# Summing the keys of a causal attention: totals folded from 128 rows to 32 by accumulating transfers, and one TensorE pass for four of them

## The chip, the cores and the metric

The kernel runs on one core of one Trainium2 chip. The metric is the device time of one execution in microseconds (us). Engines are named as in the profile: PE is TensorE, PEld its weight loads, DVE is VectorE, ACT is ScalarE, POOL is GpSimd, SP is SyncE, whose queue issues most transfers. PEclk is the clock granted to PE as a share of full speed.

## The reference

For 32 batches of 256 channels by 32x32 pixels: a group norm with 32 groups, then causal attention over the 1024 pixels with 8 heads of 32, added to the input.

```python
def reference(x, q_w, q_b, kv_w, kv_b):            # x (32, 256, 32, 32), float32
    xf = group_norm(x).reshape(B, C, S)            # 32 groups, eps 1e-5; S = 1024
    q = einsum('oc,bcs->bos', q_w, xf) + q_b       # 8 heads of 32 channels
    kv = einsum('oc,bcs->bos', kv_w, xf) + kv_b
    k, v = kv[:, :256], kv[:, 256:]                # ... to (B, 8, S, 32)
    mask = tril(ones((S, S)), -1)                  # strictly before: the centre is hidden too
    scores = where(mask == 0, -10000.0, einsum('bhqd,bhkd->bhqk', q, k) / sqrt(32))
    attn = where(mask == 0, 0.0, softmax(scores))
    return x + einsum('bhqk,bhkd->bhqd', attn, v)
```

## The kernel before

Scores are computed transposed, so that keys lie on the 128 partitions and queries along the free axis. ACT takes the exponential, POOL zeroes what the mask hides, PE multiplies with the values, and DVE adds up the exponentials of all key blocks into a running total of 128 x 4 heads x 512 queries. The softmax's denominator is the sum of that total over its 128 partitions. PE makes it with a matrix of ones (`pick`): four column blocks, one for each head of a group. A batch has four such totals (two groups of four heads, two halves of the queries; `n` counts them).

```python
        def sum_keys(pd, e, cols, of, start=True, stop=True):
            for j in range(4):
                nc.tensor.matmul(
                    pd[HD * j : HD * (j + 1), of], lhsT=pick, rhs=e[:, j, cols],
                    start=start, stop=stop, skip_group_check=True,
                )
        # ... (cut)
        def sums(b, g, hf):
            n = NH * g + hf
            total = live.pop(("sum", b, g, hf))
            # ... (the last batch's last total is cut)
            pd = misc(f"pd_{b}_{n}")
            sum_keys(pd, total, slice(0, HALF), slice(0, HALF))
            den = small.tile([P, HALF], F32, tag="den", name=f"den_{b}_{n}")
            # ... (cut)
            nc.scalar.copy(den, pd)
            if n == 0:
                live["sums", b] = dram.tile([4, 4, HALF], F32, tag="sums", name=f"sums_{b}")
            nc.sync.dma_start(out=live["sums", b][n], in_=den[::HD, :])
```

The sums go to DRAM and come back as 128 rows of 64 (`gather`), are checked and inverted, and go to DRAM and back once more, now broadcast over the 32 channels of each head (`invert`). Then DVE finishes the batch: numerator times inverse, plus bias and input.

```python
            for n in ns:                                            # in invert()
                g, hf = divmod(n, NH)
                nc.sync.dma_start(
                    out=live["rb", b][:, g, hf * HALF : (hf + 1) * HALF],
                    in_=live["inv", b][n].unsqueeze(1).broadcast_to([4, HD, HALF]),
                )
```

The order of work is laid down by hand in visits, `N = 12` to a batch. A visit does the scores of one pair of tiles, then the functions put down for it in `at`, then the values of the visit before, then the functions in `after`. POOL, PE, ACT and DVE run in exactly that order.

```python
        PREPARE = (-22, -21, -20, -19, -18, -16, -11, -11)
        SUMS = (3, 7, 9, 13)
        FINISH = (N + 7, N + 7, N + 8, N + 9)
        # ... (cut)
                if b >= 2:
                    when(max(first - 2 * N - 1, 0), lambda b=b: load(b))
                    prepare(b, [first + n for n in PREPARE])
                for n in every:
                    # ... (cut)
                    when(v, lambda b=b, n=n: sums(b, *divmod(n, NH)), after)
                if not last:
                    when(first + N + 2, lambda b=b: gather(b, every))
                    when(first + N + 4, lambda b=b: check_sums(b, every))
                    when(first + N + 4, lambda b=b: invert(b, every))
                    for n in every:
                        when(first + FINISH[n], lambda b=b, n=n: finish(b, n), after)
```

Buffers: the exponentials that become totals have three buffers of two tags each (`e0` for the first block of a total, which also holds the total), input tiles four, and one PSUM bank (`misc`) serves the key sums and the norm's small products in turn.

## Time and profile before

| | before |
|---|---|
| median of 3 runs | 1958.25 us (1957.0 to 1959.33) |
| span of the profiled run, mean PEclk | 1956.8 us, 0.998 |
| period of a batch | 60.1 us |
| PE idle in the whole span | 21.3 us (1956.8 - 1935.5) |

The table of stretches of the kernel before; columns are busy us (and instructions) of PE, PEld, DVE, ACT and POOL, then PEclk, the mean busy share of the 16 DMA engines, and GB/s:

```profile
400.00:1900.00 1500.00, 1500.00 (x18750) 746.06 (x18746) 1208.18 (x1234) 1137.28 (x1446) 455.56 (x374) 1.00 0.16 54
...
```

In the steady part PE does not stop for one microsecond in 1500, at full clock, and the DMA engines are nearly empty. The same table for two microseconds within a batch, while the four broadcasts of inverses, issued from 1068.64, are running:

```profile
1072.00:1074.00 2.00, 2.00 (x30) 0.95 (x24) 1.90 (x2) 1.34 (x2) 2.00 (x1) 1.00 0.26 100
...
```

The share stands at 0.24 to 0.29 from 1070 to 1080: a quarter of the engines' time, for ten microseconds, at some 100 GB/s. The packet records of the same trace say how: from 1070 to 1080 four packets of the broadcasts are in flight at a time, which fits four engines at work and twelve at rest.

### The profile page before, as it was taken

How to read it: one execution, taken by the hardware profiler on the slowest of the kernel's cores; microseconds unless marked ns; L12 is line 12 of the kernel's file. 1: busy time of each engine (PE TensorE's matmuls, PEld its weight loads, DVE VectorE, ACT ScalarE, POOL GpSimd, SP SyncE). 2: the span in 40 equal slices, each digit the busy share in tenths (PEclk: the TensorE clock that was granted, in tenths of full speed). 3: DMA queues.
4: the chain of work that ended last, by engine and by line, in shares of the span. 5: the costliest groups of instructions: out<-in, count | busy, mean ns of one | idle time of the engine just before them, and what ended most of it. 6: DMA issues, size and time to landing. Idle time of an engine off the chain costs nothing.

```text
span 1956.8 us, 54680 instructions
## 1 busy us (share of the span) xinstructions
PE 1935.5 (99%) x24130; PEld 964.7 (49%) x24130; DVE 1553.9 (79%) x1604; ACT 1463.6 (75%) x1865; POOL 586.0 (30%) x498
## 2 busy tenths in 40 slices
PE   8999999999999999999999999999999999999997
PEld 4454554554544545545455445454454544544543
DVE  4787887888878878888778788787887887888768
ACT  5777777777777777777777777777777777777775
POOL 1332322323323323233232232332332322323223
PEclk9999999999999999999999999999999999999999
DMA  3011111111111111111111111111111111111002
GB/s 106 3 67 42 51 57 57 67 66 38 50 53 67 68 41 52 50 64 67 50 48 53 55 67 68 36 57 47 67 67 41 52 53 61 67 57 47 32 29 78
DMA packets 56539, 107.73 MB, mean 55 GB/s; under 512 B 14064, under 2 KB 15216, under 8 KB 56296
## 3 DMA queue, kind: packets, MB, share of 16 engines
q1 hardware_dynamic: 54520, 103.26, 14.8%
q8 instruction: 191, 3.13, 0.7%
q10 hardware_dynamic: 1776, 0.92, 0.2%
q14 instruction: 52, 0.43, 0.1%
HBM read 68.54 MB, written 35.62 MB: 53 GB/s over the span
## 4 chain that ended last, share of the span: by engine, by line
PE 97%; DVE 2%; DMA 1%; ACT 0%; issue 0%; ACTq 0%; SPq 0%; DVEq 0%
PE sT L267 30%; PE acc L337 25%; PE pp L159 24%; PE ppv L159 12%; PE pd L351 6%; DVE e L342 0%; DMA wn<-in_L_conv_kv_w_dram 0%; DMA x<-in_x_dram 0%; DVE rb L439 0%; PE pv L159 0%; DVE rb L422 0%; DVE rb L423 0%; PE pm L159 0%; ACT e L314 0%; ACT k L221 0%
## 5 line engine op out<-in xcount | busy, mean ns | idle before, releaser
L314 ACT ACTIVATE e<-sT 128x1024 f32<-128x1024 f32 x768 | 744.9, 1022 | 274.0 <-PE sT L267 227.6
L342 DVE TENSOR_TENSOR e<-e,eh 128x1024 f32<-128x1024 f32 x382 | 540.0, 1427 | 361.2 <-PE acc L337 341.1
L282 POOL TENSOR_SCALAR_AFFINE_SELECT e<-e 128x512 f32<-128x512 f32 (+1 forms) x256 | 392.9, 1535 | 1337.5 <-ACT e L314 1151.9
L342 DVE TENSOR_TENSOR e<-e,e 128x1536 f32<-128x1536 f32 x381 | 634.0, 1664 | 17.4 <-POOL e L282 3.0
L267 PE MATMUL sT<-q,k 32*128 32x256 f32 (+3 forms) x7168 | 617.5, 460 | 0.8 <-ACT k L221 0.8
L267 PEld LDWEIGHTS sT<-q,k 32*128 32x128 f32 x7168 | 463.6, 184 | 202.3 <-issue 105.6
L159 PE MATMUL pp<-xn,wT 128*32 128x512 f32 x4096 | 492.2, 598 | 0.0
L337 PE MATMUL acc<-e,v 128*32 128x512 f32 (+2 forms) x4096 | 400.7, 486 | 0.0
L315 ACT ACTIVATE eh<-sT 128x1024 f32<-128x1024 f32 x384 | 396.2, 1032 | 0.0
L159 PE MATMUL ppv<-wT,xn 128*32 128x256 f32 x4096 | 247.3, 382 | 0.0
L337 PEld LDWEIGHTS acc<-e,v 128*32 128x32 f32 x4096 | 132.6, 110 | 223.1 <-issue 200.7
L337 PE MATMUL acc<-eh,v 128*32 128x256 f32 x3072 | 224.4, 379 | 0.0
L159 PEld LDWEIGHTS pp<-xn,wT 128*32 128x32 f32 x4096 | 107.0, 109 | 218.2 <-issue 206.2
L382 ACT COPY den<-pd 128x512 f32<-128x512 f32 x126 | 73.9, 586 | 165.1 <-PE pd L351 165.1
L337 PEld LDWEIGHTS acc<-eh,v 128*32 128x32 f32 x3072 | 98.5, 110 | 164.2 <-issue 152.6
L159 PEld LDWEIGHTS ppv<-wT,xn 128*32 128x32 f32 x4096 | 120.2, 109 | 102.0 <-issue 32.1
L282 POOL TENSOR_SCALAR_AFFINE_SELECT eh<-eh 128x512 f32<-128x512 f32 x128 | 163.3, 1276 | 2.8
L351 PE MATMUL pd<-e,pick 128*32 128x512 f32 (+1 forms) x1048 | 136.7, 595 | 2.0 <-DVE e L342 2.0
L423 DVE SCALAR_TENSOR_TENSOR rb<-rb,v_bias_col,x 128x512 f32<-128x512 f32 (+1 forms) x127 | 95.4, 751 | 4.5
L221 ACT ACTIVATE q<-pp,qk_bias 128x512 f32<-128x512 f32 x128 | 89.9, 702 | 3.9 <-PE pp L159 3.9
L221 ACT ACTIVATE k<-pp,qk_bias 128x512 f32<-128x512 f32 x128 | 89.8, 702 | 2.2 <-PE pm L159 1.1
L346 ACT COPY num<-acc 128x512 f32<-128x512 f32 x128 | 76.4, 597 | 15.6 <-PE acc L337 15.6
(62 smaller groups left out, 526.2 us busy)
## 6 DMA issues: line engine op xcount, KB each, us to landing
x<-in_x_dram SPq DMA_DIRECT2D x64, 512.0 KB
out_dram<-rb SPq DMA_DIRECT2D x127, 256.0 KB
rb<-inverses SPq DMA_DIRECT2D x126, 256.0 KB
sums<-den SPq DMA_DIRECT2D x126, 8.0 KB
rows<-sums SPq DMA_DIRECT2D x31, 32.0 KB
inverses<-inv SPq DMA_DIRECT2D x31, 32.0 KB
wn<-in_L_conv_kv_w_dram ACTq DMA_DIRECT2D x2, 256.0 KB
wn<-in_L_conv_q_w_dram ACTq DMA_DIRECT2D x1, 256.0 KB
```

The costliest lines, as they stand in the source:

```text
L159: nc.tensor.matmul(out[part], lhsT=lhsT[:, part], rhs=rhs, start=start, stop=stop, skip_group_check=True)
L221: nc.scalar.activation(live[key][:, cols], pp, AF.Identity, bias=qk_bias[:, n, g : g + 1], scale=(SCALE, 1.0)[n],)
L267: ins = nc.tensor.matmul(pair[:, cols], lhsT=live["k", b, g][rows, kb * P : (kb + 1) * P], rhs=live["q", b, g][rows, hf * HALF + of.start ...
L282: nc.gpsimd.affine_select(out=diagonal, in_=diagonal, pattern=[[0, 4], [0, n], [1, P]], compare_op=ALU.is_gt, fill=0.0, base=0, channel_mu ...
L314: nc.scalar.activation(e[:, 2 * a : 2 * a + 2, :], pairs[a], AF.Exp)
L315: exp = nc.scalar.activation(eh.rearrange("p (n bank) q -> p bank n q", n=2), short, AF.Exp)
L337: nc.tensor.matmul(acc[HD * j : HD * (j + 1), of], lhsT=live["v", b][:, kb, h * HD : (h + 1) * HD], rhs=e[:, j, cols], start=first, stop=l ...
L342: nc.vector.tensor_add(total[:, :, of], total[:, :, of], e[:, :, cols])
L346: nc.scalar.copy(live["num", b][:, g, hf * HALF : (hf + 1) * HALF], acc)
L351: nc.tensor.matmul(pd[HD * j : HD * (j + 1), of], lhsT=pick, rhs=e[:, j, cols], start=start, stop=stop, skip_group_check=True,)
L382: nc.scalar.copy(den, pd)
L423: nc.vector.scalar_tensor_tensor(rb[:, g, cols], rb[:, g, cols], v_bias_col[:, g : g + 1], xt[:, g, cols], ALU.add, ALU.add)
```

## The change

The intent is to take three of the four PE groups of a batch away. GpSimd issues two transfers for each total that add its upper 64 rows to its lower 64, then the upper 32 of those to the lower 32 (`accum_op=ALU.add`). SP copies the 32 remaining rows into a stacked tile of 128 rows. With a matrix that picks by blocks of 32 rows (`pick_half`), one PE group sums all four totals at once. Everything behind moves later by three visits, and so do, to keep the buffers alive, the loads and the norm by two.

```diff
+        def fold(b, n, rows):
+            total = live["sum", b, *divmod(n, NH)]
+            nc.gpsimd.dma_start(out=total[:rows], in_=total[rows : 2 * rows], accum_op=ALU.add)
+
+        def stack(b, n):
+            if n == 0:
+                live["folded", b] = work.tile([P, 4, HALF], F32, tag="folded", bufs=1, name=f"folded_{b}")
+            total = live.pop(("sum", b, *divmod(n, NH)))
+            nc.sync.dma_start(out=live["folded", b][n * HD : (n + 1) * HD], in_=total[:HD])
+
+        def sum_folded(b):
+            pd = misc(f"pd_{b}")
+            sum_keys(pd, live.pop(("folded", b)), slice(0, HALF), slice(0, HALF), of_rows=pick_half)
+            # ... (copy to den, one write of 16 rows to DRAM)
 ...
-        PREPARE = (-22, -21, -20, -19, -18, -16, -11, -11)
+        PREPARE = (-20, -19, -18, -17, -16, -14, -11, -11)
-        FINISH = (N + 7, N + 7, N + 8, N + 9)
+        FINISH = (N + 10, N + 10, N + 11, N + 12)
 ...
-                    when(max(first - 2 * N - 1, 0), lambda b=b: load(b))
+                    when(max(first - 2 * N + 1, 0), lambda b=b: load(b))
 ...
+                        when(v, lambda b=b, n=n: fold(b, n, 2 * HD), after)
+                        when(v + 1, lambda b=b, n=n: fold(b, n, HD), after)
+                        when(v + 2, lambda b=b, n=n: stack(b, n), after)
 ...
-                    when(first + N + 2, lambda b=b: gather(b, every))
-                    when(first + N + 4, lambda b=b: check_sums(b, every))
-                    when(first + N + 4, lambda b=b: invert(b, every))
+                    when(first + N + 4, lambda b=b: sum_folded(b), after)
+                    when(first + N + 5, lambda b=b: gather(b, every), after)
+                    when(first + N + 7, lambda b=b: check_sums(b, every))
+                    when(first + N + 7, lambda b=b: invert(b, every))
```

(The last batch keeps its four groups.)

More of the change, by code (lines that the diff above doesn't have):

```diff
@@ L75, in tile_norm_attention_residual @@
     nc.gpsimd.memset(pick, 1.0)
+    pick_half = const.tile([P, 4, CPG], F32, name="pick_half")
+    nc.gpsimd.memset(pick_half, 1.0)
+    nc.gpsimd.affine_select(
+        out=pick_half, in_=pick_half, pattern=[[-HD, 4], [0, CPG]],
+        compare_op=ALU.is_ge, fill=0.0, base=0, channel_multiplier=1,
+    )
+    nc.gpsimd.affine_select(
+        out=pick_half, in_=pick_half, pattern=[[HD, 4], [0, CPG]],
+        compare_op=ALU.is_ge, fill=0.0, base=HD - 1, channel_multiplier=-1,
+    )
+    pick_half = pick_half.rearrange("p a b -> p (a b)")
     avg = const.tile([P, P // CPG, CPG], F32, name="avg")
@@ L346, in values, with sum_keys @@
                 nc.scalar.copy(live["num", b][:, g, hf * HALF : (hf + 1) * HALF], acc)
-        def sum_keys(pd, e, cols, of, start=True, stop=True):
+        def fold(b, n, rows):
[9 more added lines that the diff above has]
+            sum_keys(pd, live.pop(("folded", b)), slice(0, HALF), slice(0, HALF), of_rows=pick_half)
+            den = small.tile([P, HALF], F32, tag="den", name=f"den_{b}")
+            nc.scalar.copy(den, pd)
+            live["sums", b] = dram.tile([4, 4, HALF], F32, tag="sums", name=f"sums_{b}")
+            nc.sync.dma_start(out=live["sums", b].rearrange("j n c -> (j n) c"), in_=den[::CPG, :])
+        def sum_keys(pd, e, cols, of, start=True, stop=True, of_rows=pick):
             for j in range(4):
                 nc.tensor.matmul(
-                    pd[HD * j : HD * (j + 1), of], lhsT=pick, rhs=e[:, j, cols],
+                    pd[HD * j : HD * (j + 1), of], lhsT=of_rows, rhs=e[:, j, cols],
                     start=start, stop=stop, skip_group_check=True,
@@ L375, in sums @@
             den = small.tile([P, HALF], F32, tag="den", name=f"den_{b}_{n}")
-            if b == B - 1 and n >= 2:
+            if n >= 2:
                 most = small.tile([P, 1], F32, tag="most", name=f"most_{n}")
@@ L410, in invert @@
                 live["rb", b] = work.tile([P, NG, S], F32, tag="rb", name=f"rb_{b}")
+            by_half = live["inv", b] if b == B - 1 else live["inv", b].rearrange("j n c -> n j c")
             for n in ns:
@@ L414, in invert @@
                     out=live["rb", b][:, g, hf * HALF : (hf + 1) * HALF],
-                    in_=live["inv", b][n].unsqueeze(1).broadcast_to([4, HD, HALF]),
+                    in_=by_half[n].unsqueeze(1).broadcast_to([4, HD, HALF]),
                 )
@@ L432, in check_here @@
             least = small.tile([P, 1], F32, tag="least", name=f"least_{n}")
-            junk = small.tile([P, HALF], F32, tag="junk", bufs=1, name=f"junk_{n}")
+            junk = small.tile([P, HALF], F32, tag="den", name=f"junk_{n}")
             nc.vector.tensor_scalar(junk, live["den", n], SUM_MIN, 1.0, ALU.is_ge, ALU.min, accum_out=least)
@@ L549, in unshifted @@
                             when(first + i, lambda b=b, i=i: sum_pieces(b, products[i - 1], i == N - 1, i == N), after)
-                    when(v, lambda b=b, n=n: sums(b, *divmod(n, NH)), after)
+                    if last:
+                        when(v, lambda b=b, n=n: sums(b, *divmod(n, NH)), after)
+                    else:
+                        when(v, lambda b=b, n=n: fold(b, n, 2 * HD), after)
+                        when(v + 1, lambda b=b, n=n: fold(b, n, HD), after)
+                        when(v + 2, lambda b=b, n=n: stack(b, n), after)
                 if not last:
-                    when(first + N + 2, lambda b=b: gather(b, every))
-                    when(first + N + 4, lambda b=b: check_sums(b, every))
-                    when(first + N + 4, lambda b=b: invert(b, every))
+                    when(first + N + 4, lambda b=b: sum_folded(b), after)
+                    when(first + N + 5, lambda b=b: gather(b, every), after)
+                    when(first + N + 7, lambda b=b: check_sums(b, every))
+                    when(first + N + 7, lambda b=b: invert(b, every))
                     for n in every:
```

## The prediction

> **What bounds the kernel now.** I read first the page's busy shares, then the chain that ended last, then its costliest groups, to see which engine sets the pace and what part of it the change touches:
>
> ```profile
> PE 1935.5 (99%) x24130; PEld 964.7 (49%) x24130; DVE 1553.9 (79%) x1604; ACT 1463.6 (75%) x1865; POOL 586.0 (30%) x498
> ...
> PE 97%; DVE 2%; DMA 1%; ACT 0%; issue 0%; ACTq 0%; SPq 0%; DVEq 0%
> ...
> L382 ACT COPY den<-pd 128x512 f32<-128x512 f32 x126 | 73.9, 586 | 165.1 <-PE pd L351 165.1
> L351 PE MATMUL pd<-e,pick 128*32 128x512 f32 (+1 forms) x1048 | 136.7, 595 | 2.0 <-DVE e L342 2.0
> ```
>
> PE is busy for 99% of the span and is 97% of the chain, so time taken off PE comes off the end unless something else begins to make PE wait. The key totals (pd) are 1048 matmul instructions: 131 groups of eight (four column blocks, each product two instructions), almost one group per quarter of a batch. 136.7 us is their busy time, which overlaps their neighbours'. The chain in order of time counts what a group adds to the end; its summary gives 5.8% of 1956.8 us = 113.5 us, over 131 groups 0.87 us, and a single piece agrees:
>
> ```profile
> 1902.61 1.72 PE acc L337 x24
> 1904.33 0.86 PE pd L351 x8
> 1905.19 1.50 PE sT L267 x12
> ```
>
> A batch is 12 visits (scores of one visit, values of the one before, then extra work). The timeline of SP's queue shows its period, 1085.59 - 1025.48 = 60.1 us:
>
> ```profile
> 1025.48 5.69 SPq L428 DMA_DIRECT2D out_dram<-rb  x3
> ...
> 1036.63 1.81 SPq L106 DMA_DIRECT2D x<-in_x_dram  x2
> ...
> 1085.59 5.69 SPq L428 DMA_DIRECT2D out_dram<-rb  x3
> ```
>
> Less the four groups (3.5 us) and the two tiny norm groups that is about 4.67 us a visit, as the PE timeline also has it: visit 12 of a batch starts at 1043.39 and visit 13 at 1048.05.
>
> **What the Trainium skill says.** "DMA: Bandwidth & Descriptors", section "SWDGE vs HWDGE vs iDMA", has accumulation during a transfer only from GpSimd, which writes the descriptors in software; that is why the folds sit in GpSimd's queue, among the masks. The kernel before issues none there, so no row prices it. The same page, "Anatomy of one DMA", fits such a transfer as 2.0 us + bytes/436e3; for 512 KB that is 3.2 us, for 256 KB 2.6 us, without the accumulation. In the loop of this trace only SP issues transfers: the small write of the inverses, issued at 1067.03, let its reader issue at 1068.64, so 1.6 us there and back; and in one-microsecond windows the two 512 KB loads moved up to 418 GB/s, which agrees. "SBUF — State Buffer", section "Who interferes with whom", says that a DVE instruction with two SBUF inputs contends with a GpSimd instruction that reads SBUF but not with one that only writes. This trace agrees with the first half: one mask shape (128x512) took from 0.68 to 2.58 us in one batch. The second half says that the adds should not starve descriptor writing; no run here shows it yet. "TensorE: Matmul & The Clock Gate", Part 3, says that products in different column groups run together; a pd group of eight instructions of 0.59 us each lasts 1.04 us, which agrees, and the new pass keeps the form.
>
> **The change part by part.**
> 1. Removed from PE: of the 131 groups, 31 batches lose four and gain one. The compiled order has 93 fewer PE rows, one per group, and the last batch keeps its own. 93 x 0.87 = **81 us off the path**.
> 2. Removed from ACT: 93 copies of 586 ns, 54 us off an engine at 75%; beside the path. Four small writes to DRAM per batch become one of 16 rows, from SP, beside the path.
> 3. Added to GpSimd: 8 issues a batch, 248 in all. An issue costs an estimated 1 us (no row shows it; taken below the two-microsecond fixed part above): 8 us on 18.3 us of masks in a 57 us batch, far from full. Each second fold waits in GpSimd's order for the first to land. In the compiled order only the second folds of the first and third total have a mask before them and the next mask a visit behind; the others fall in the two-visit gap without masks (14 us idle in the trace). So masks should not be late.
> 4. Added to DMA: per total 512 + 256 KB of folding and 256 KB of stacking; 124 totals make 130 MB, on 107.7 MB now. The engines were 16% busy, so some 30 to 40%; not a bound, but the x loads and outputs now meet the folds.
> 5. Moved on DVE: the four finishes go from visits 7, 7, 8, 9 after the next batch starts to 10, 10, 11, 12, where adds already crowd. The DVE timeline in the stretch that produces the fourth total:
>
> ```profile
> 1032.47 2.36 DVE L342 TENSOR_TENSOR e<-e,eh 128x1024 f32<-128x1024 f32 x2 [1.65 <-PE acc L337]
> 1034.75 0.68 DVE L422 TENSOR_TENSOR rb<-num,rb 128x512 f32<-128x512 f32 x1
> 1035.46 0.75 DVE L423 SCALAR_TENSOR_TENSOR rb<-rb,v_bias_col,x 128x512 f32<-128x512 f32 x1
> 1036.13 2.29 DVE L342 TENSOR_TENSOR e<-e,e 128x2048 f32<-128x2048 f32 x1
> 1038.52 1.51 DVE L342 TENSOR_TENSOR e<-e,eh 128x1024 f32<-128x1024 f32 x1
> 1040.14 2.29 DVE L342 TENSOR_TENSOR e<-e,e 128x2048 f32<-128x2048 f32 x1
> 1042.53 1.93 DVE L342 TENSOR_TENSOR e<-e,eh 128x1024 f32<-128x1024 f32 x1
> 1044.57 3.24 DVE L342 TENSOR_TENSOR e<-e,e 128x1536 f32<-128x1536 f32 x2
> 1047.91 1.51 DVE L342 TENSOR_TENSOR e<-e,eh 128x1024 f32<-128x1024 f32 x1
> ```
>
> It is unbroken from 1032.47 to 1049.42. One finish (1.43 us) leaves it and three (each 1.43, with one 0.15 copy) enter ahead of the last add, +3.0 us: the fourth total ends near 1052.5 on this clock. PE's visit 14 would begin at 1048.05 + 4.67 = 1052.7 on the same clock, less the one removed group between them, 0.9 us. So the total is done about **0.7 us into visit 14**.
> 6. The new chain that PE waits for: first fold, second fold, stack, then the single pass after visit 16, 3 x 4.67 = 14.0 us after visit 14 starts. My estimates: first fold 1 us of issue + 1.3 to 2.6 us of movement (512 KB at 418 GB/s, or twice for reading the target too) + 1.5 us to be seen = 3.8 to 5.1; second 3.1 to 3.8; stack on SP 0.5 + 0.6 + 1.5 = 2.6. Sum 9.5 to 11.5, and 1 to 2.5 more where the 1 MB of x loads runs in the same microseconds: 10.5 to 14 after a start at 0.7. It fits with **0 to 3 us to spare**, on the edge; I put down 0.4 us a batch, 31 x 0.4 = 12 us.
> 7. The tail: from 1920.9 the chain is DVE alone, 31 us, with the finishes of batch 30 in it. Moving these later leaves DVE idle first and loaded after; up to the 6.1 us of four finishes is added, I take 5 us.
>
> Sum: 1958 - 81 + 12 + 5 = 1894; as the author's offsets look fitted to these waits, I shade it to **1890 us**.
>
> **The rivals.** (a) *The fold chain ends late and PE waits for the stacked tile.* For: the margin of step 6, the crowded DVE, one in-order SP queue that puts the stack behind outputs and loads. Against: the pass stands one visit after the stack. Each microsecond late costs 31 us; 2.6 us late eats the whole gain, so 1920 to 1990. (b) *GpSimd becomes the wait*: if an issue takes 3 us or more, or DVE starves it, masks come late, and PE has only some 1 to 2 us between a mask's end and the values that need it (a mask of visit 5 ends at 1015.60, PE uses it at 1016.53). Two late masks a batch of 1 us: 62 us, 1940 to 1950. (c) *DVE becomes the bound*: 1554/1890 = 82% on average, but visits 10 to 12 now carry about 6.9, 5.7 and 6.2 us in 4.67. It recovers in the light visits 13 to 15, and three buffers give about two visits of slack; so a few us at most. (d) *The gain is hidden anyway*: PE is 97% of the chain, so no. (e) Everything fits and the tail costs nothing: 1958 - 81 = 1877, or 1870 if a group is worth the 0.94 us that starts of neighbours differ by at one place.
>
> **Range and chances.** (e) is the floor, 1868. (a) and (b) in moderate form give the upper end, 1940. Faster by over 2% is below 1919: 36 us of losses beyond the 1877 + 5, 1.2 us a batch. I think three in four that the waits stay under it: 0.75; within 2%: 0.17; slower: 0.08.
>
> **What would show it.** Right: pd matmuls fall from 1048 to 304, den copies from 126 to 126 - 93 = 33, PE still above 97% and pd about 1.8% of the chain. Step 6: PE's idle before pd, released by the stacking transfer, is the loss; under 15 us in total confirms it, 80 us is rival (a). Step 3: idle of PE before values released by the masks on GpSimd is rival (b), and GpSimd's issues over 3 us. Step 5: the last add of the fourth total should end within visit 14. Step 7: the DVE chain at the end longer than 31 us. It would be wrong mainly through the duration of an accumulating transfer, which nothing in this trace measures.

## The result, and the profile after

| | before | after |
|---|---|---|
| median of 4 runs | 1958.79 us (1957.0 to 1959.45) | 2084.43 us (2073.88 to 2085.4) |
| profiled span, mean PEclk | 1956.8 us, 0.998 | 2082.7 us, 0.968 |
| PE idle in the span | 21.3 us | 162.9 us |
| period of a batch | 60.1 us | 59.8 to 65.2 us |

The change made the kernel slower: ratio 1.0631, 95% interval 1.0596 to 1.0666. A ratio here is always the mean time of one kernel's fast runs over the mean of the other's of the same rounds, so not quite the ratio of the medians. The prediction, 1890 us in 1868 to 1940, was wrong. The output was correct.

The page of the changed kernel: busy shares, the queue of the folds (packets, MB, share of 16 engines), the chain that ended last, a group, and two rows of issues (KB each, median us from issue to landing):

```profile
PE 1919.8 (92%) x23386; PEld 964.2 (46%) x23386; DVE 1567.8 (75%) x1604; ACT 1407.8 (68%) x1772; POOL 711.9 (34%) x749
...
q0 software_dynamic: 15872, 97.53, 33.8%
...
PE 44%; issue 22%; DMA 18%; POOL 9%; DVE 4%; ACT 3%; POOLq 0%; SPq 0%; ACTq 0%; DVEq 0%
...
L365 POOL DMA_DIRECT2D e<-e x248 | 204.1, 880 | 730.7 <-DMA e<-e 573.5
...
e<-e POOLq DMA_DIRECT2D x124, 512.0 KB, 8.6
...
e<-e POOLq DMA_DIRECT2D x124, 256.0 KB, 4.8
```

PE has fallen from 97% of the chain to 44%, and transfers carry 18%. The first folds land 8.6 us after their issue, the second ones 4.8 us (medians of all four totals). PE does 744 instructions less but is busy only 15.7 us less, which is odd for groups worth 81 us; the clock explains it below. PE's waits, with total us, times, and the longest:

```profile
PE pd L384 <- issue: 60.8, 18, 4.2
PE pd L384 <- DMA folded<-e: 40.1, 13, 4.2
PE acc L349 <- POOL e L294: 11.4, 28, 1.0
```

All 31 passes over the stacked tile wait (18 and 13), together 101 us. Where the label is "issue" the profile shows no releaser, but it is the same instruction, and it reads a tile that the stacking transfer fills. One batch shows the length of the road to it. On DVE the last add of the fourth total, then POOL's two folds of it, then SP with its neighbours, then PE (start, duration, engine and instruction, the idle time before and its releaser):

```profile
1044.08 2.14 DVE L354 TENSOR_TENSOR e<-e,eh 128x1024 f32<-128x1024 f32 x1
```

```profile
1046.52 0.89 POOL L365 DMA_DIRECT2D e<-e  x1 [1.38 <-DVE e L354]
1053.37 0.78 POOL L365 DMA_DIRECT2D e<-e  x1 [5.96 <-PE ppv L171]
```

```profile
1048.02 3.54 SPq L118 DMA_DIRECT2D x<-in_x_dram  x2
1058.92 0.51 SPq L371 DMA_DIRECT2D folded<-e  x1
```

```profile
1045.57 1.57 PE L279 MATMUL sT<-q,k 32*128 32x256 f32 x16
...
1058.99 0.61 PE L349 MATMUL acc<-eh,v 128*32 128x256 f32 x8
1063.03 1.23 PE L384 MATMUL pd<-folded,pick_half 128*32 128x512 f32 x8 [3.43 <-issue]
1064.20 3.09 PE L279 MATMUL sT<-q,k 32*128 32x256 f32 x24
```

The total is ready at 1046.22 and the first fold issued at 1046.52. The second fold follows 6.85 us later, the stack 5.55 us after that, and PE starts the pass 4.11 us after the stack: 16.5 us in all (medians of the 31 batches: 7.0, 5.0 and 4.5, and 16.4 from the first issue to the pass). PE was ready at 1059.60, 14.0 us after its visit 14 began at 1045.57. (POOL's second wait bears the name of a PE product; in other batches the same row, with the same length, names the first fold's landing.) Two more things are to be seen. The three transfers have neighbours: the loads of the next input are issued 1.5 us behind the first fold, and the first fold of the next batch's first total (at 1056.84, cut here) 2.1 us ahead of the stack. And after the gap, the score products that take 1.67 us elsewhere in this batch take 3.09 us. The table of stretches has the clock there (columns as before: busy us of PE, PEld, DVE, ACT and POOL, then PEclk, share, GB/s):

```profile
1063.80:1067.20 3.40, 3.40 (x28) 2.66 (x24) 3.00 (x5) 1.39 (x2) 0.00 (x0) 0.50 0.57 64
```

"TensorE: Matmul & The Clock Gate" of the Trainium skill, Part 1, "What's actually happening", has PE's clock drop to half after an idle window of about 3.4 us, free-running. The clock records of this trace agree with the half and with the free-running window: before the end of the program there are 21 stretches at 0.50, each 3.41 or 6.83 us long, and their starts lie whole multiples of 3.41 us apart. They do not show that the gap itself must be that long: 21 of the 31 gaps at the pass were followed by such a stretch, gaps from 2.8 to 4.2 us; the other gaps were 1.1 to 3.3 us (the ends of PE's instructions, and so the lengths of gaps, are modelled). The prediction did not have this term at all: a wait of this length can be paid twice.

At the end of the program, DVE of the changed kernel:

```profile
2044.78 0.22 DVE L433 SCALAR_TENSOR_TENSOR in_range<-rows,in_range 64x64 f32<-64x64 f32 x1 [12.65 <-DMA rows<-sums]
```

The last batch's small write of sums stands behind the late steps of the batch before it, and DVE waits 12.65 us for it; in the kernel before there is no such wait.

### The profile page after: what moved, and what is told of

It is laid out like the page before. It is cut to its first block, busy times and chain, and to the rows that moved or that the text cites. A ratio compares the mean times of both kernels' runs of the same rounds, so it can differ in the third digit from the quotient of the medians.

```text
span 2082.7 us, 53914 instructions
## 1 busy us (share of the span) xinstructions
PE 1919.8 (92%) x23386; PEld 964.2 (46%) x23386; DVE 1567.8 (75%) x1604; ACT 1407.8 (68%) x1772; POOL 711.9 (34%) x749
## 3 DMA queue, kind: packets, MB, share of 16 engines
q0 software_dynamic: 15872, 97.53, 33.8%
## 4 chain that ended last, share of the span: by engine, by line
PE 44%; issue 22%; DMA 18%; POOL 9%; DVE 4%; ACT 3%; POOLq 0%; SPq 0%; ACTq 0%; DVEq 0%
PE sT L279 15%; DMA e<-e 12%; PE acc L349 12%; PE pp L171 10%; POOL e L294 5%; PE ppv L171 5%; DMA folded<-e 4%; ACT e L326 3%; DVE e L354 2%; PE pd L384 2%; POOL e L365 2%; POOL rstd L209 1%; POOL eh L294 1%; DMA sums<-den 1%; DVE rb L457 1%
## 5 line engine op out<-in xcount | busy, mean ns | idle before, releaser
L354 DVE TENSOR_TENSOR e<-e,eh 128x1024 f32<-128x1024 f32 x382 | 509.3, 1347 | 382.0 <-PE acc L349 227.1
L279 PE MATMUL sT<-q,k 32*128 32x256 f32 (+3 forms) x7168 | 646.1, 477 | 0.9 <-ACT k L233 0.8
L279 PEld LDWEIGHTS sT<-q,k 32*128 32x128 f32 x7168 | 487.0, 193 | 183.1 <-issue 60.5
L294 POOL TENSOR_SCALAR_AFFINE_SELECT e<-e 128x512 f32<-128x512 f32 (+1 forms) x256 | 320.9, 1254 | 589.8 <-ACT e L326 580.3
L365 POOL DMA_DIRECT2D e<-e x248 | 204.1, 880 | 730.7 <-DMA e<-e 573.5
L349 PE MATMUL acc<-e,v 128*32 128x512 f32 (+2 forms) x4096 | 401.5, 487 | 11.4 <-POOL e L294 11.4
L294 POOL TENSOR_SCALAR_AFFINE_SELECT eh<-eh 128x512 f32<-128x512 f32 x128 | 145.8, 1139 | 4.6 <-ACT eh L327 3.6
L384 PE MATMUL pd<-folded,pick_half 128*32 128x512 f32 x248 | 44.2, 787 | 101.0 <-issue 60.8
L378 ACT COPY den<-pd 128x512 f32<-128x512 f32 x31 | 18.2, 586 | 153.2 <-PE pd L384 153.2
L456 DVE TENSOR_TENSOR rb<-num,rb 128x512 f32<-128x512 f32 (+1 forms) x127 | 115.5, 909 | 0.1
L457 DVE SCALAR_TENSOR_TENSOR rb<-rb,v_bias_col,x 128x512 f32<-128x512 f32 (+1 forms) x127 | 105.4, 830 | 4.5
```

The lines of the kernel that those rows point to most:

```text
L279: ins = nc.tensor.matmul(pair[:, cols], lhsT=live["k", b, g][rows, kb * P : (kb + 1) * P], rhs=live["q", b, g][rows, hf * HALF + of.start ...
L294: nc.gpsimd.affine_select(out=diagonal, in_=diagonal, pattern=[[0, 4], [0, n], [1, P]], compare_op=ALU.is_gt, fill=0.0, base=0, channel_mu ...
L349: nc.tensor.matmul(acc[HD * j : HD * (j + 1), of], lhsT=live["v", b][:, kb, h * HD : (h + 1) * HD], rhs=e[:, j, cols], start=first, stop=l ...
L354: nc.vector.tensor_add(total[:, :, of], total[:, :, of], e[:, :, cols])
L365: nc.gpsimd.dma_start(out=total[:rows], in_=total[rows : 2 * rows], accum_op=ALU.add)
L384: nc.tensor.matmul(pd[HD * j : HD * (j + 1), of], lhsT=of_rows, rhs=e[:, j, cols], start=start, stop=stop, skip_group_check=True,)
```

## The experiments

Twelve runs, each with rounds against the kernel before on the same chip. The first theory was: PE's wait for the stacked tile, with the slow clock behind it, is the loss (the prediction's rival (a)). Its rival: the rest of the change (transfers, masks, moved places) is.

### The pass without its wait

The stacked tile is still made, but PE sums a tile of ones instead, so the result is wrong.

```diff
-            sum_keys(pd, live.pop(("folded", b)), slice(0, HALF), slice(0, HALF), of_rows=pick_half)
+            live.pop(("folded", b))
+            for j in range(4):
+                nc.tensor.matmul(pd[HD * j : HD * (j + 1), :], lhsT=pick_half,
+                                 rhs=ones.broadcast_to([P, HALF]), start=True, stop=True, ...)
```

> The changed kernel, but the single pass reads a constant of ones instead of the stacked tile (a wrong result on purpose). All folds, stacks and their traffic stay; PE alone no longer waits for them. Theory A (PE's wait for the fold chain, with the slow clock after it, is the loss): the batch period falls from 63.8 us to about 60.1 - 2.6 = 57.5, plus some 0.4 us for one late mask; the clock is back at 0.99 or more; with the tail still some 19 us longer, 1958 - 81 + 19 + 12 = 1908 us. Theory B (traffic, GpSimd or DVE crowding slow the kernel by themselves): stays above 2000 us.

Measured: 1940.96 us (1934.39 to 1955.33), ratio 0.9935 (0.9893 to 0.9978), clock 0.991. All 101 us of waits are gone and the time falls by 143 us. So the wait and what follows from it make up nearly all of the loss. The expected 1908 was not reached: 33 us are lost otherwise. Of 29 periods 16 now take 57.9 to 58.1 us, which is the period of before, 60.1, less three groups of 0.87, plus about 0.4; **the removed groups are worth what the prediction said**. The other periods take 58.6 to 60.3 us and one 65.1 us, with a gap of 4.45 us in it; together they are 22 us above 57.9 each, and why is not known. The ends cost more, which the runs below show.

### The moved places alone

The kernel before with only the new places of loads, norm, gather, check, inversion and finishes; no fold, no stack, four groups. Correct.

```diff
-        PREPARE = (-22, -21, -20, -19, -18, -16, -11, -11)
+        PREPARE = (-20, -19, -18, -17, -16, -14, -11, -11)
-        FINISH = (N + 7, N + 7, N + 8, N + 9)
+        FINISH = (N + 10, N + 10, N + 11, N + 12)
   (load, gather, check_sums, invert moved as in the change)
```

> The kernel before with only the changed kernel's places of the later steps (loads and norm two visits later, gathering, checking, inverting and finishing three visits later); four PE groups a batch, no folds. Theory: the crowding of DVE by the moved finishes costs nothing in the steady state (PE busy 100% and a period of 60.1 us as before), but the end of the program grows, because the last batch's small write of sums now falls beside the broadcasts of the batch before it; in the changed kernel the time from the last single pass to the end was some 19 us longer. So 1970 to 1980 us, all of the increase after about 1890 us. Rival: the moved finishes delay PE every batch: PE idle in the middle, 1990 us or more.

Measured: 1993.32 us, ratio 1.0181 (1.0164 to 1.0198), above the expected band; the places alone cost 34.6 us. PE's waits name the first part, DVE's the second:

```profile
PE pv L159 <- ACT k L221: 11.7, 31, 0.4
```

```profile
DVE in_range L400 <- DMA rows<-sums: 12.4, 1, 12.4
```

Once a batch a tiny product of the norm (pv) now comes right behind a projection that holds the shared PSUM bank, and waits 0.38 us until ACT has emptied it: 12 us over the program. And the end stretches: with the batch before last finishing three visits later, its broadcasts stand ahead of the last batch's small write, and DVE waits 12.4 us. So, against the expectation, not all of the increase lies at the end: the key sum that PE starts at 1904.2 us in the kernel before starts at 1923.3 here, 19 us later, and 15 us more are lost behind it. (Beside the 12 us, PE waits six times in the steady part for the last add of a total, 4.4 us in all.) The mean clock, 0.994 where before has 0.998, adds little to it: of 24.7 us at half clock, all at the end, PE was busy in 3.5.

### Work for PE in the gap

Three groups whose result is overwritten, placed right ahead of the pass. Correct.

```diff
+            for _ in range(3):
+                for j in range(4):
+                    nc.tensor.matmul(pd[HD * j : HD * (j + 1), :], lhsT=pick, rhs=wT[:, 0, :HALF],
+                                     start=True, stop=True, skip_group_check=True)
             sum_keys(pd, live.pop(("folded", b)), ..., of_rows=pick_half)
```

> The changed kernel with three groups of useless matmuls (3 x 0.87 = 2.6 us) on PE in front of the single pass, into the same bank, which the pass then overwrites. They fill part of the wait and lengthen nothing where the wait is longer than 2.6 us. Theory: the wait of some 4 us empties PE long enough for the clock to drop, and the slow stretch after it costs about 60 us in all (mean clock 0.968 against 0.998). Filled, the clock stays at 0.995 or more, and the time falls to about 2020 to 2030 us although PE does more. Rival (the low clock is noise of the chip or has another cause): clock stays near 0.97 and the time at 2080 or above.

Measured: 2046.54 us (2043.81 to 2047.67), ratio 1.0452, clock 0.993. Giving PE 31 x 2.6 = 81 us **more** to do makes the kernel 38 us **faster** (medians; 36 by the means). The wait left at the pass is 22.7 us in sum (these and 1.2 named "issue"), the longest 2.0:

```profile
PE pd L390 <- DMA folded<-e: 21.5, 26, 2.0
```

No stretch at half clock is left before the end of the program, and the mean clock is 0.993 against 0.968. The useless groups take the place of 78 us of waiting almost one for one, so this shows the second payment: some 38 us of the loss are the slow clock after the gap. The time missed the expected 2020 to 2030 by 17 us and the clock the expected 0.995 by 0.002.

### Folds that copy instead of adding

The same transfers, from the same queue, without the accumulation. Its output is wrong, which doesn't matter for the time.

```diff
-            nc.gpsimd.dma_start(out=total[:rows], in_=total[rows : 2 * rows], accum_op=ALU.add)
+            nc.gpsimd.dma_start(out=total[:rows], in_=total[rows : 2 * rows])
```

(The check of the sums is made to pass, and the inverse is taken of ones.)

> The changed kernel with both folds as plain copies of the same bytes from the same queue, not accumulating (wrong result on purpose; the check on the sums is made to pass and the inverse is taken of ones, so that all stays finite). Theory A1 (the adding itself slows the transfer: 5.7 us of engine time per total in the trace where plain transfers moved 299 GB/s): the first fold lands in 5 us instead of 8.6, the second in 3.5 instead of 4.8, the stack is then in time for PE, 1900 to 1915 us. Theory A2 (the software issue and the queueing are the latency, not the adding): landing stays above 7.5 us and the time above 2040 us.

Measured: 2065.54 us, ratio 1.0541 (1.0523 to 1.0558). The adding costs the engines much: the page has the software queue's share at 22.4% of 16 engines where it was 33.8%, for the same bytes. For an 8 KB row that is 0.62 us against 0.95 us of an engine's time (0.224 x 16 x 2072.6 us, and 0.338 x 16 x 2082.7 us, over 97.53 MB / 8 KB = 11,905 rows). But the time hardly moves, which looks as if adding did not matter. The timeline of one batch, POOL and SP:

```profile
1036.61 0.57 POOL L365 DMA_DIRECT2D e<-e  x1 [1.37 <-DVE e L354]
1042.03 0.50 POOL L365 DMA_DIRECT2D e<-e  x1 [4.86 <-DMA e<-e]
```

```profile
1038.11 3.22 SPq L118 DMA_DIRECT2D x<-in_x_dram  x2
1048.29 0.51 SPq L371 DMA_DIRECT2D folded<-e  x1
```

The first fold takes 5.4 us, not 6.85, so the second begins sooner and runs full beside the input's loads: 6.3 us from its issue to the stack, where it had taken 5.55. What the first step gained the second lost; over all batches more so than in this one (medians 5.2 and 7.8 us, where the changed kernel has 7.0 and 5.0).

### The loads out of the way

The changed kernel (adding folds) with the input's loads issued by ACT's queue, four visits later, and the norm two visits later. Correct.

```diff
-                nc.sync.dma_start(out=live["x", b][:, g, :], in_=x_in[b, :, g, :])
+                (nc.scalar if b >= 2 else nc.sync).dma_start(out=live["x", b][:, g, :], in_=x_in[b, :, g, :])
-                    when(max(first - 2 * N + 1, 0), lambda b=b: load(b))
+                    when(first - 2 * N + 5, lambda b=b: load(b))
-        PREPARE = (-20, -19, -18, -17, -16, -14, -11, -11)
+        PREPARE = (-18, -17, -16, -15, -14, -12, -11, -11)
```

> The changed kernel (correct result) with the loads of x issued by ACT at visit 17, after the single pass, instead of by SP at visit 13; bn and norm two visits later. That takes 1 MB of traffic out of the stretch in which the fourth total is folded. Theory: the chain of first fold, second fold and stack shortens from 16.5 us (6.9 + 5.5 + 4.1 in one batch of the trace) to 12 to 13.5, PE's wait before the pass from about 4 us to under 1, the clock comes back; period 58 to 59 us and 1920 to 1940 us. Rival (the transfers are slow by themselves, whoever runs beside them): the chain stays above 15 us and the time above 2030 us.

Measured: 2051.07 us (2041.43 to 2061.22), ratio 1.0477. My theory of that moment, that the loads alone make the folds late, fell: the rival's figure was right. PE still waits 89.7 us at the pass, this and 19.3 us named as the stack's landing:

```profile
PE pd L384 <- issue: 70.4, 25, 4.1
```

Moving the loads gained 33 us, but the chain is only one microsecond shorter: in the median of the batches the first fold takes 6.1 us, the second 4.7 and the stack 4.6, and the whole 15.4 where the changed kernel has 16.4. The stack still has a neighbour, the first fold of the next batch's first total; in the worst batch that fold is issued 0.8 us ahead of it, the stack takes 6.3 us and the whole 17.1.

### Both together

Plain copies and loads out of the way; wrong.

```diff
 the edits of the two runs above, both
```

> The plain-copy kernel (wrong on purpose) with the loads moved in the same way. With plain copies alone the first fold of the fourth total fell from 6.9 to 5.4 us but the second then ran beside the loads and rose to 6.2, so nothing was gained. If contention and adding both count, this one is fastest of the three: chain 10 to 11.5 us, no wait before the pass, 1905 to 1930 us. If it equals the kernel with the moved loads alone within 1%, the adding does not matter once the loads are gone.

Measured: 1950.1 us (1948.67 to 1955.04), ratio 0.9964, clock 0.992. The time missed the expected band by 20 us, but the wait at the pass is gone: 6.7 us in all. One batch on POOL:

```profile
1036.70 0.57 POOL L365 DMA_DIRECT2D e<-e  x1
1041.51 0.50 POOL L365 DMA_DIRECT2D e<-e  x1 [4.24 <-DMA e<-e]
```

The stack is issued at 1044.83 and PE starts the pass at 1049.81, on its own time. The three steps take 4.8, 3.3 and at most 5.0 us, 13.1 at most, under the 14.0 that PE gives. Medians over the batches of the four kernels, fourth total, in us:

| | first fold to second | second to stack | stack to pass | first fold to pass |
|---|---|---|---|---|
| changed kernel | 7.0 | 5.0 | 4.5 | 16.4 |
| plain copies | 5.2 | 7.8 | 3.1 | 16.2 |
| loads away | 6.1 | 4.7 | 4.6 | 15.4 |
| both | 4.8 | 2.9 | 5.4 at most | 13.3 at most |

So two causes make the chain late, and taking either away alone leaves one that is still too long for the 14.0 us: **the adding makes each fold slower** (third row against fourth: some 1.2 us on the first fold and 1.8 on the second), **and the loads move at the same time** (second row against fourth). The other neighbour, the next batch's first fold beside the second fold or the stack, was there in all four; no run removed it. Where the 20 us go that this run misses its band by was not followed; its periods are 58.2 to 61.5 us, so most of them lie in the steady part.

### Three totals folded, the fourth left to PE

The fourth total is the only one whose folds are urgent. PE sums it as before, into the same bank, behind the pass over three. Correct; 62 groups fewer instead of 93.

```diff
-            sum_keys(pd, live.pop(("folded", b)), ..., of_rows=pick_half)
+            sum_keys(pd, live.pop(("folded", b))[: 3 * HD], whole, whole, True, False, of_rows=pick_half[: 3 * HD])
+            sum_keys(pd, live.pop(("sum", b, NG - 1, NH - 1)), whole, whole, False, True, of_rows=pick_last)
 ...
-                    else:
+                    elif n < 3:
                         when(v, lambda b=b, n=n: fold(b, n, 2 * HD), after)
```

> Correct result. Only the first three totals of a batch are folded and stacked; the fourth, whose chain is the late one, is added by a second PE group from its own 128 rows into the same bank. PE then runs two groups a batch instead of four: 62 x 0.87 = 54 us less than before. Theory A: PE's wait before the pass vanishes (the third stack has landed about two visits earlier), period about 58.4 us, clock 0.99, and with a tail of 19 us about 1925 us (1915 to 1940). Theory B (traffic or GpSimd order slow the kernel by themselves): above 1990 us.

Measured: 1966.49 us (1964.48 to 1967.6), ratio 1.004, clock 0.993. The wait at the pass is gone, but the expected 1925 is missed by 41 us. PE is idle for 26 us between 400 and 1900. The waits name masks:

```profile
PE acc L352 <- POOL e L297: 19.4, 28, 2.5
```

And POOL's timeline says why the masks are late:

```profile
1016.37 0.84 POOL L368 DMA_DIRECT2D e<-e  x1
1026.85 1.61 POOL L368 DMA_DIRECT2D e<-e  x2 [9.63 <-DMA e<-e]
```

POOL works in order. Its next instruction, a fold, waits 9.63 us for the fold before to land, and the masks stand behind it. The slow fold, issued at 1016.37, runs beside the four broadcasts that SP issued at 1015.53, the ten microseconds on a quarter of the engines that the second table of "before" showed. The packet records show the meeting: sampled once a microsecond, the fold has 12 packets in flight from 1018.5 to 1020.5, none at 1021.5 and 1022.5, and 4 at most from 1023.5 to 1025.5. Its share on the four engines of the broadcasts comes last.

### The pass two visits earlier

With no urgent fold left, the pass and the steps behind it can stand earlier, and the loads and the norm at their old places. Correct.

```diff
-        FINISH = (N + 10, N + 10, N + 11, N + 12)
+        FINISH = (N + 8, N + 8, N + 9, N + 10)
-                    when(first + N + 4, lambda b=b: sum_folded(b), after)
+                    when(first + N + 2, lambda b=b: sum_folded(b), after)
   (gather, check_sums, invert two visits earlier; load and PREPARE as before the change)
```

> Correct result. Three totals folded, the fourth added directly, as before in the run with two groups, but with the single pass two visits earlier (after visit 14) and the later steps only one visit later than in the kernel before. The two-group kernel lost 1.1 us a batch to masks held up on GpSimd behind a fold that ran beside the broadcasts, and some 19 us at the end. With the earlier places the broadcasts fall beside the first total's folds, which have time. Period 58.4 to 59 us, end as before: 1958 - 54 + 5 to 15 = 1909 to 1925 us. If the traffic of the folds costs PE in any case, it stays at 1950 or above.

Measured: 2280.85 us, ratio 1.1648: the largest miss. ACT's first wait, and SP in one batch:

```profile
ACT e L329 <- DMA folded<-e: 352.0, 30, 12.7
```

```profile
1031.24 2.51 SPq L452 DMA_DIRECT2D rb<-inverses  x4
1033.93 2.56 SPq L374 DMA_DIRECT2D folded<-e  x1
```

Now the stack of the first total is issued right behind the four broadcasts and lands some 17 us later, when ACT goes on at 1050.95 (the median over all stacks is 11.7 us). Until then it holds one of the three `e0` buffers, and the exponential that needs it waits up to 12.7 us, and PE behind it up to 9.4 us.

### The broadcasts over all engines

"DMA: Bandwidth & Descriptors" of the Trainium skill, section "Why a DMA increments its semaphore by 16 and not by 1", says that a transfer is spread over the largest number of engines up to 16 that divides the slowest dimension of both sides. The broadcast reads 4 rows, so four engines by that rule, and the share of 0.26 in the kernel before agrees. Written as four transfers of 32 partitions each, the rule gives 16. First as a control in the kernel before, then in the last two kernels; all correct.

```diff
-                nc.sync.dma_start(
-                    out=live["rb", b][:, g, hf * HALF : (hf + 1) * HALF],
-                    in_=by_half[n].unsqueeze(1).broadcast_to([4, HD, HALF]),
-                )
+                for j in range(4):
+                    nc.sync.dma_start(
+                        out=live["rb", b][HD * j : HD * (j + 1), g, hf * HALF : (hf + 1) * HALF],
+                        in_=by_half[n][j : j + 1].broadcast_to([HD, HALF]),
+                    )
```

> The kernel before with one edit: each broadcast of the inverses (one transfer in which a 128-partition target reads 4 rows) written as four transfers of 32 partitions. Correct. Control for the two split runs: nothing waits for these broadcasts in the steady state of the kernel before, so all theories expect 1958 us within 0.5 % (1949 to 1968). If it is slower than that, the extra issues on SP cost something by themselves and the others must be read against it.

> The run 'three' (three totals folded, the fourth added by PE) with each broadcast of the inverses written as four transfers. Correct. Theory: the broadcasts of a batch occupied only four of the sixteen DMA engines for some 10 us, the first folds of the next batch meet them there, GpSimd stands in order behind the folds and its masks are late; spread over the engines they pass quickly, the masks are on time, and the wait for the small write of the sums at the end shrinks: 1910 to 1940. Rival: the transfers' engines are not what slows the folds (it is the adding itself): 1960 to 1970 as 'three'.

> The run 'early' (three totals folded, the pass two visits earlier, the later steps one visit later than in the kernel before) with each broadcast written as four transfers. Correct. 'early' lost 320 us because a stack stood behind the four broadcasts for 17 us and held a buffer that the next exponential needed. If it was the crowding of four engines, the stacks land in under 8 us and the time falls to 1905 to 1950. Rival: the stack is late whatever the form of the broadcasts, because it shares SP's queue with them: over 2150.

Measured: the control 1958.83 us, ratio 1.0002 (0.9985 to 1.0018), so the broadcasts are hidden there in either form; in it they move 138 to 145 GB/s at shares of 0.42 to 0.50 instead of 100 at 0.26, with 7 to 10 packets in flight; SP needs 7.3 us to issue the sixteen. With three totals folded: 1929.63 us (1929.37 to 1930.04), ratio 0.9857 (0.984 to 0.9873), 37 us less than with the old form, as expected. With the early pass: 2083.55 us, ratio 1.0628; 197 us come back, but the band of 1905 to 1950 is missed.

The run with three totals and split broadcasts, steady part, and its first folds on the page:

```profile
400.00:1900.00 1500.00, 1487.49 (x18698) 750.62 (x18691) 1233.98 (x1251) 1116.77 (x1402) 529.17 (x531) 1.00 0.52 107
...
```

```profile
e<-e POOLq DMA_DIRECT2D x93, 512.0 KB, 5.9
```

First folds land in 5.9 us where they took 9.0 in the run with the old broadcasts (medians of three totals together). It is the second total's fold that gained, the one beside the broadcasts: 10.2 to 5.9 us. The third total's stays slow, 9.0 and 8.7 us, and harms nothing here. PE is at full clock, and every batch takes 58.8 us: 60.1 less two groups (1.74) plus the 0.4 of the norm's product. So the gain of the groups now shows. The early pass shows the limit of the cure: the stacks land in 6.0 us instead of 11.7, but ACT still waits 181 us for them. The place of the stack behind the broadcasts in SP's order and the three buffers are as before; which of the two holds it was not tested.

### The end of the program

The last run with three totals and split broadcasts, but the batch before last handled as in the kernel before: its four totals summed by PE one at a time, its steps at the old visits. Correct.

```diff
-                    if last:
+                    if last or old:                      # old = (b == B - 2)
                         when(v, lambda b=b, n=n: sums(b, *divmod(n, NH)), after)
 ...
+                if old:
+                    (gather at N + 2, check_sums and invert at N + 4, finishes at N + 7, 7, 8, 9)
+                elif not last:
```

> The run 'split3' with the last batch but one handled as in the kernel before (four totals summed by PE one at a time, its gather, check, inversion and finishes at the old visits), so that nothing of it stands ahead of the last batch's small writes. Correct. Theory: what is left between split3's 1930 us and the 1903 that 62 groups fewer would give is mostly the end of the program, where the late steps of the last batch but one pile up (in split3 PE waits 5.0 us for the last total and 8.8 us for the check, both on DVE): two groups more cost 2 us and 12 to 20 come back, 1912 to 1920. Rival: the end is slow because of the split broadcasts or the folds of the steady state, and the time stays at 1928 to 1932.

Measured: 1920.69 us (1918.95 to 1921.28), ratio 0.9805 (0.9789 to 0.9821), clock 0.998. Two groups more, and 9 us less; just above the expected 1912 to 1920. DVE's wait for the small write has shrunk from 8.9 us in the run without this edit (three waits, the longest 8.4, at the end) to:

```profile
DVE in_range L438 <- DMA rows<-sums: 0.9, 1, 0.9
```

This version is correct and beats both kernels: 38 us below the kernel before and 164 us below the changed one. (Whether it is faster than before by more than 2% is open: the interval lies on both sides of 0.98.)

## Why the prediction was wrong, by its own steps

**Step 6 failed, and it decided the outcome.** It put the first fold at 3.8 to 5.1 us, the second at 3.1 to 3.8 and the stack at 2.6, with up to 2.5 more for the loads, 10.5 to 14 in all; the batch shown measured 6.85, 5.55 and 4.11 = 16.5 (median 16.4). The window of 14.0 us was right to the tenth (1045.57 to 1059.60). The margin it gave, 0 to 3 us, was by its own numbers -0.7 to 2.8 (14.0 less the start at 0.7 and less 10.5 to 14). An error of 2.5 us beyond its upper end turned 0.4 us a batch into a wait of 101 / 31 = 3.3 us. The estimates came from the rate of loads running alone (418 GB/s) and from the skill's fit for a transfer without adding. The runs show two terms that were too small, and only with both removed the wait goes (13.3 us at most): the adding, which with the loads away costs some 1.2 us on the first fold and 1.8 on the second, and the loads in the same engines. The text named the first as its main risk, and gave the second at most 2.5 us; with plain copies it took 2.9 us or more (16.2 less 13.3).

**A term was missing: the clock.** The prediction priced a late tile at 31 us per microsecond. Of the 31 gaps 21 also threw PE to half speed for the products behind them. The filler run shows some 38 us of this. The clock records give an estimate of 47 us: before the end of the program PE was busy in 93.3 us at half clock, and half of that was lost. The busy time agrees: for the same instructions it is 1919.8 us here and 1874.6 us in the run without the wait, 45 us less. It is why PE's busy time fell by only 15.7 us against the kernel before.

**Step 1 was right.** 93 groups of 0.87 us: pd went from 1048 to 304 instructions, and 16 of 29 batches of the run without a wait took 57.9 to 58.1 us, 2.6 - 0.4 below before. **Step 2 was right:** the copies of `den` fell from 126 to 33, and ACT is 3% of the chain.

**Step 3 was right on the issue and half right on the masks.** An issue took 0.88 us (estimate 1). But masks were late 28 times for 11.4 us in all, not because issuing is long but because POOL stands in order behind the wait for the first fold's landing (9.63 us in the batch of the run with three totals); the prediction had seen that order and judged the masks safe with folds of 4 to 5 us.

**Step 4 was too small and wrong in conclusion.** The engines' share was estimated at 30 to 40% and came out at 59% in the steady part; the rows that add take half as long again as those that copy (0.95 against 0.62 us). More to the point, "not a bound" was read from an average; four packets in flight at a time for ten microseconds, with the other engines empty, were in the trace of before, and I did not look at the window.

**Step 5 was right.** The fourth total was ready 0.65 us into visit 14 (0.7 predicted).

**Step 7 was too small.** It allowed 5 us (at most 6.1) for the end. The moved places alone make DVE wait 12.4 us there for a small write; undoing them for one batch gave back 9 us net of two groups. And the norm's product that waits 0.38 us a batch for the shared bank, 12 us in all, was in no step.

**The sum.** The groups and the moved places are shown by runs of their own: 1958.7 - 81 (groups) + 34.6 (moved places, their end and norm wait included) = 1912 us. The run without the wait took 1941, so 29 us are open. From there to the changed kernel are 143 us, measured, for PE's wait and all that follows from it. The traces offer 101 us (the wait), 47 (slow clock) and 11 (late masks, of which the run without the wait keeps 0.5) for them, together 159; so these parts overlap by some 16 us, and their split is an estimate.

Of the rivals, (a) came true with the size beyond its range of 1920 to 1990, because the slow clock and the end came on top; (b) came true in a small way; (c) hardly (PE's 4.4 us for last adds in the run of the moved places); (d) and (e) did not occur. In the ranges, 0.75 for faster was too much for a step said to be on the edge whose main duration nothing in the trace measured.

**What stays open.** The 29 us of the run without the wait: 22 of them are its longer periods, whose cause was not followed. In the run with plain copies and the loads away, what takes the periods to 58.2 to 61.5 us was not followed either. No run took away the next batch's first fold, which runs beside the end of the chain.

## What to carry to other kernels

A mean share of the DMA engines says nothing about a latency chain: look at the windows in which your transfer will run, who else moves there, and over how many engines each neighbour is spread. If a chain of transfers takes the place of work on the bounding engine, give it its slowest measured duration or leave its last link out: three of four totals with room to spare beat all four at the edge. And a wait on PE can cost twice: 21 of the 31 waits here, of 2.8 to 4.2 us, were followed by products at half clock.

## What the Trainium skill lacked or had wrong

- "DMA: Bandwidth & Descriptors", "Anatomy of one DMA": the fit (2.0 us + bytes/436e3) gives 3.2 us for 512 KB and 2.6 us for 256 KB. The fastest plain copies within SBUF landed after 4.1 and 2.8 us, so the fit is close for the smaller one alone; the page does not say that adding takes longer, and the fastest adding folds of all runs landed after 5.1 and 4.5 us. In the traffic of the changed kernel the medians were 8.6 and 4.8.
- The same page, "SWDGE vs HWDGE vs iDMA", says who may accumulate, not at what rate: 0.95 us of an engine's time for an 8 KB row that adds, 0.62 us for one that copies. An issue on GpSimd took 0.82 us in the median for a fold that adds and 0.52 us for one that copies.
- The same page has the rule for how many engines a transfer uses, and warns that a broadcast can be confined to few; it does not say what that does to others. Here: four packets in flight, 100 GB/s for ten microseconds, and the first fold beside it at 10.2 us instead of 5.9.
- "SBUF — State Buffer", "Who interferes with whom": nothing wrong found. That adds on DVE do not starve the writing of descriptors, which the page infers, agrees: an issue of the changed kernel took 0.81 us in the median under an add on DVE (135 issues) and 0.79 with DVE idle (11).
- "TensorE: Matmul & The Clock Gate", Part 1, was right on the half clock and the free-running window (3.41 us in the clock records). It asks for a whole idle window of about 3.4 us; here gaps from 2.8 us in the changed kernel, and one of 2.4 us with plain copies, were enough by the profile's modelled ends. It does not say that filling such a gap with useless products can pay, which here gave 38 us.
